# W's low pieces by VectorE, P7's bank in halves, another first load order, in a factorization kernel of seven products

## The chip, the cores and the metric

The kernel runs on one core of a Trainium2 chip. The metric is the device time of one execution in microseconds, the median of several. The core has TensorE for matrix products (PE in the profile, its weight loads PEld), VectorE (DVE), ScalarE (ACT), GpSimd (POOL) and SyncE (SP), each with an instruction stream of its own, and 16 DMA engines that they share. SBUF is the on-chip memory; PSUM is the small memory into which TensorE writes, in banks.

## The reference

A factorization machine: a linear layer and, for each of 512 outputs, the pairwise interaction of 64 embeddings. All of it is float32.

```python
# x 1024x512, weight 64x512x512, lin_w 512x512, lin_b 512
out_lin = x @ lin_w.T + lin_b
xv = jnp.einsum('bf,efm->bem', x, weight)
zp = jnp.einsum('bf,efm->bem', jnp.square(x), jnp.square(weight))
interaction = 0.5 * jnp.sum(jnp.square(xv) - zp, axis=1)
return out_lin + interaction
```

The second product needs no einsum of its own: summed over the embeddings it is x² times the column sums of W², one product of the size of the linear layer.

## The kernel before, in words

**Seven products.** Each large product is cut into 2 x 2 blocks and computed with seven products of blocks instead of eight. P1 to P7 are these products; X's operands are the blocks A11, A12, A22 and the sums R5, R6, R7, R3 (`OPERAND`), W's are the blocks w11, w21, w22, a sum w12 that takes w22 in, and T, which takes in one more block for each of P5, P6 and P4 (`RHS`, `load_more`, L596). There are 32 stages h, two for each of 16 groups of embeddings, and seven products in each. `ORDER = (1, 6, 2, 3, 7, 5, 4)` is their order within a stage, where 5 belongs to the next one.

**Three passes.** TensorE's full fp32 product is slow, its fp32r form is faster but cuts the operands. So `split` (L612) makes three pieces of a block of W: H, the block scaled and cut; L, what H leaves of it; K, a difference of the two. `x_pieces` (L471) does the same with X, once. A product is H by H and L by L, the "front" (8 matmuls of 128x512 for a half), then an operation on the bank that scales it and adds what another product left (`stt`, L349, or a scaling at L712), then the "back", K by K (4 matmuls), which TensorE's order puts `LAG = 4` slots later. In the first stage the products in `PLAIN` are done in fp32, without pieces. A product has two halves, each in a bank pair of its own out of four.

**Who makes a piece.** H is always a copy by ScalarE (`act`, L343), K a GpSimd operation (`pool`, L361). L is, by the table `SPLIT`, either a ScalarE copy and a GpSimd subtraction ("POOL"), or a ScalarE copy and an accumulating DMA that GpSimd issues ("DMA"), or one VectorE operation on two SBUF operands.

**The ends of a product.** P1 and P5: ScalarE copies the bank to p1 or p5. P6: VectorE makes w = bank + p5 (`dve`, L355). P2, P3, P4, P7: `finish` (L663): ScalarE squares the bank, VectorE reduces the squares over the embeddings of the stage into `acc` (L368). P7 also gives w = bank - p5, which P4 needs. The squares of W are ScalarE's `wsq` and a VectorE reduction `w_sum`. After every second stage the sums are transposed and stored.

**Head and tail.** The linear layer goes first, through the same seven products in fp32 (`one_level`, L485; P1 and P2 by `by_k`, L494, the rest L507), behind loads of x (`load_x`, SyncE's queue) and lin_w (`load_lw`, most on ScalarE's queue) and four matmuls of zeros. Then W's stages begin with P5 of stage 0. The tail is the product of x² with the sums of W², again by `one_level`, with VectorE adding the banks into the output tiles (`into`, L833).

**What sets the order.** The program is a list of operations with reads and writes. `Plan.forward` (L140) walks it with the cost of each operation (`plan.add`) and gives every engine a fixed order: TensorE by the keys (slots) of the products, the others by the latest time at which an operation may end, SyncE's loads no sooner than `AHEAD` before that. `Plan.order` (L117) repeats the walk `ROUNDS` times with changed deadlines and keeps the best. VectorE operations whose operands both lie in SBUF are marked `both`; the planner lets them and GpSimd's tensor operations take turns, and where it held one back the order between the two engines is made a dependency. DMAs of W's blocks are issued by SyncE (L375), accumulating ones by GpSimd (L380).

Of the kernel before, what the change touches and what calls it, by code (L numbers as in the profile page):

```python
# [33 lines left out]
PE, DVE, ACT, POOL, SP = "PE", "DVE", "ACT", "POOL", "SP"  # L34
# [3 lines left out]
class Plan:  # L38
    HOP = 0.3
    OWN = 0.05  # L40
    AHEAD = 50.0
    ROUNDS = 60
    SEED = 0
    DEPTH = 8
    YIELD = 0.0

# [27 lines left out]
    def deadlines(self, chain):  # L74
# [11 lines left out]
        while stack:  # L86
            o = stack.pop()
            latest = t if o.latest is None else o.latest
            cost = min(o.costs.values()) + o.move + o.land + self.HOP
# [50 lines left out]
    def forward(self, chain):  # L140
# [6 lines left out]
        done, late, nxt, wire, held = [], 0.0, 0, [9.0], None  # L147
# [5 lines left out]
        def ready(o, e=None):  # L153
            at = self.HOP
            for d in o.deps:
                own = ops[d].engine == e and not ops[d].move
                at = max(
                    at, ops[d].end + (self.OWN * (e != PE) if own else self.HOP * (e != NONE))
                )
            return at  # L160

        def ends(e, o, at):
            free[e], o.end, running[e] = at, at + o.land, o
# [3 lines left out]
            for t in (at, o.end, o.end + self.OWN, o.end + self.HOP):  # L167
                heapq.heappush(times, t)
# [6 lines left out]
        def pick(e, now):  # L175
# [23 lines left out]
        while len(done) < len(ops):  # L199
            now = heapq.heappop(times)  # L200
            moved = True
            while moved:
                moved = False
                for e in pending:
# [9 lines left out]
                    if e == PE:  # L214
                        nxt += 1
                        late = max(late, now - o.latest)
                    cost = o.costs[e]
                    o.start, o.engine = now, e
                    tensor = e == POOL and not o.move
                    if e == DVE and o.both and free[POOL] > now + 0.05 and not running[POOL].move:  # L220
                        held, free[e], o.end = o, float("inf"), float("inf")
                    elif tensor and held is not None and held.latest < o.latest + self.YIELD:
                        ends(DVE, held, now + held.costs[DVE])
                        o.after, held = held, None
                        ends(e, o, o.after.end + self.HOP + cost)
# [15 lines left out]
def kernel(  # L241
# [7 lines left out]
):  # L249

# [90 lines left out]
    def act(o, i, func, reads, writes, size=1024, scale=1.0, bias=0.0):  # L341
# [3 lines left out]
        plan.add({ACT: 0.14 + 0.92 * size / 1024}, emit, reads, writes)  # L345

    def stt(o, i, scalar, j, op, reads, writes, size=512, both=False, cost=None):
# [3 lines left out]
        plan.add({DVE: cost or 0.14 + 1.08 * size / 1024}, emit, reads, writes, both=both)  # L351

    def dve(o, a, b, sub, reads, writes, size=512, both=False):
# [3 lines left out]
        plan.add({DVE: 0.14 + 1.08 * size / 1024}, emit, reads, writes, both=both)  # L357

    def pool(o, a, b, sub, reads, writes, size=1024):
# [3 lines left out]
        plan.add({POOL: 0.15 + 2.35 * size / 1024}, emit, reads, writes)  # L363

    def reduce(o, i, reads, writes):
        plan.add(
            {DVE: 1.21},
# [6 lines left out]
    def dma(o, i, reads, writes, move=1.75, on=(SP,)):  # L374
        plan.add(dict.fromkeys(on, 0.45), lambda e: queues[e].dma_start(o, i), reads, writes,  # L375
                 land=2.0, move=move)

    def dma_add(o, i, reads, writes, move=2.75):
        plan.add(
            {POOL: 0.95}, lambda _: nc.gpsimd.dma_start(o, i, accum_op=ALU.add),  # L380
            tuple(reads) + tuple(writes), writes, land=2.5, move=move,
        )
# [20 lines left out]
    def load_x(n, k, lo, hi, at):  # L403
        r, q = quads[n]
        half = H // 2
        nc.sync.dma_start(
            buf[n][:, k, lo * half:hi * half],
            x_src[:, q * KH + k, r * H + lo * half:r * H + hi * half],
        )
        for u in range(lo, hi):  # L410
            landing((n, k, u), at)
# [9 lines left out]
    load_x("A11", 0, 0, 1, 3.5)  # L421
    load_lw(nc.scalar, [0], 0, 3.5)
    load_x("A11", 0, 1, 2, 3.9)
    load_lw(nc.scalar, [1], 0, 5.2)
    load_x("A11", 1, 0, 2, 5.0)
    load_lw(nc.scalar, [2, 3], 0, 7.2)
    load_x("A12", 0, 0, 2, 6.4)
    load_x("A12", 1, 0, 2, 7.4)
    load_lw(nc.sync, [0, 1], 1, 8.4)
    load_lw(nc.sync, [2, 3], 1, 9.2)  # L430
    for at, (n, k) in enumerate((("A22", 0), ("A22", 1), ("A21", 0), ("A21", 1))):
        load_x(n, k, 0, 2, 10.0 + 0.8 * at)
    nc.scalar.dma_start(bias[:], lin_b)
    landing("bias", 9.5)
    nc.scalar.preload_act_table(AF.Square)

    def a_parts(*names):
        return tuple((n, k, u) for n in names if n in quads for k in range(KH) for u in range(2)) + tuple(
# [46 lines left out]
    def one_level(p, rhs, left, bank, first, key, by_k=False):  # L485
# [3 lines left out]
        if by_k:  # L489
            for at, (u, k) in enumerate(steps):  # L490
                for half in range(2):
                    def emit(_, u=u, k=k, half=half):
                        cols = slice(half * H // 2, (half + 1) * H // 2)
                        nc.tensor.matmul(  # L494
                            buf[bank[u]][:, cols], b[:, k, ts(u, P)], a[:, k, cols],
                            start=first and k == 0 and half == 0, stop=k == KH - 1,
                            skip_group_check=True,
                        )

                    names = (a_names[2 * k + half],) + (b_names[k],)  # L500
                    plan.add({PE: WHOLE / 2}, emit, names + (bank[u],), (bank[u],),
                             key=key + 0.1 * at + 0.05 * half)
            return
        for u in range(2):
            def emit(_, u=u):
                for k in range(KH):
                    nc.tensor.matmul(  # L507
                        buf[bank[u]], b[:, k, ts(u, P)], a[:, k, :], start=first and k == 0,
                        stop=k == KH - 1, skip_group_check=True,
                    )  # L510

# [8 lines left out]
    f1, f4, f3, f2 = four()  # L520
# [32 lines left out]
    one_level(6, lin_rhs, lhs, f2, False, -960)  # L553
# [5 lines left out]
    lin_copy("L12", f2, 1, -1.0)  # L559
# [3 lines left out]
    one_level(7, lin_rhs, lhs, f2, False, -940)  # L563
    lin_add("L22", f2, True)
    lin_store("L22", 1, 1)
    lin_add("L21", f2, False)
# [29 lines left out]
    def load_more(h, n, q):  # L596

        o = now[h, n]
        if h:
# [28 lines left out]
    def prepare(h, p):  # L628
# [28 lines left out]
        return n if not h and p in PLAIN else split(n, SPLIT[p] if h else POOL)  # L657
# [5 lines left out]
    def finish(h, p, half, bank):  # L663
        row, col = {2: (0, 0), 3: (0, 1), 4: (1, 0), 7: (1, 1)}[p]
        sq, a = square(), acc_name[h // NCB]
        act(buf[sq], buf[bank], AF.Square, both_of(bank), (sq,))
        m, b = (2 * col + h % NCB) * MI, row * NJ + 2 * half
        reduce(buf[a][:, b:b + 2, m:m + MI], buf[sq], (sq,), ((a, b // 2, m),))

    def product(h, p):  # L670
        ops, plain = prepare(h, p), not h and p in PLAIN
        for half in range(2):
# [3 lines left out]
            def mm(x, w, j, first, bank=bank, half=half):  # L676
                for k in range(KH):
                    nc.tensor.matmul(buf[bank, j], buf[x][:, k, ts(2 * half + j, P)],  # L678
                                     buf[w][:, k, :], start=first and k == 0, stop=k == KH - 1,
                                     skip_group_check=True)  # L680

            addend = {6: "p1", 2: "p1", 3: "w", 7: "w", 4: "w"}.get(p)
# [236 lines left out]
```

## Time and profile before

| what | value |
|---|---|
| three runs | 1297.63, 1298.60, 1299.33 us (median 1298.6) |
| profiled execution | 1299.58 us, its span 1297.6 us |
| mean granted TensorE clock | 0.999 of full speed |
| matmuls (PE) | 1280.1 us busy, 99%, x5484 |
| VectorE (DVE) | 1086.7 us, 84%, x954 |
| ScalarE (ACT) | 1011.9 us, 78%, x1071 |
| GpSimd (POOL) | 1095.3 us, 84%, x590 |
| DMA | 200.25 MB; GpSimd's queue 101.72 MB |

The span runs from the first to the last instruction; the time of the execution has 2.0 us more. A row of a group has the line, engine, operation, tiles written and read, the number of instructions after x, and then busy time, mean duration in ns, and idle time before it with the releaser. A DMA row gives the queue, the number, KB of each and the median time from issue to landing. A record of TensorE is one pass over 512 columns; an fp32 matmul has two records. DVE durations run over the start of the next instruction by about 0.1 us, so the distance of two starts is what an operation costs on its engine.

### The profile page before, as it was taken

To read this page: it belongs to the slowest core of one execution; us is meant where nothing else is said; L and a number is where in the kernel's file an instruction comes from. 1 tells how busy PE (TensorE), PEld (TensorE's weight loads), DVE (VectorE), ACT (ScalarE), POOL (GpSimd) and SP (SyncE) were. 2 spreads that over 40 slices of the span, in tenths; PEclk is the share of its full clock that TensorE was granted. 3 is DMA by queue.
4 is the path that set the end of the run, shared out by engine and by line. 5 is a ranking of instruction groups with operands and counts; after the bars stand their busy time and mean duration, and the time that the engine had idled before them with its cause. 6 is when DMAs were issued, how large, how long until landed. Compare 5 with 4: busy or idle time off the path is not lost.

```text
span 1297.6 us, 15705 instructions
## 1 busy us (share of the span) xinstructions
PE 1280.1 (99%) x5484; PEld 1026.0 (79%) x5484; DVE 1086.7 (84%) x954; ACT 1011.9 (78%) x1071; POOL 1095.3 (84%) x590
## 2 busy tenths in 40 slices
PE   8999999999999999999999999999999999999997
PEld 4668888888888888888888888888888888888873
DVE  4699888888888888888888888888888889888884
ACT  5568788788777888877888887788888788888872
POOL 3659898898888899889889888888988888998891
PEclk9999999999999999999999999999999999999999
DMA  6366676757667666677766666767667676766866
GB/s 226 97 164 160 155 170 150 158 129 154 163 155 167 142 152 145 149 163 164 162 147 143 153 151 161 167 145 161 133 148 168 147 162 152 169 131 144 184 130 150
DMA packets 75998, 200.25 MB, mean 154 GB/s; under 512 B 23824, under 2 KB 25104, under 8 KB 75920
## 3 DMA queue, kind: packets, MB, share of 16 engines
q0 software_dynamic: 28512, 101.72, 44.0%
q1 hardware_dynamic: 45552, 94.91, 22.6%
q10 hardware_dynamic: 1856, 2.62, 0.6%
q8 instruction: 43, 0.70, 0.2%
q14 instruction: 35, 0.29, 0.1%
HBM read 158.34 MB, written 6.29 MB: 127 GB/s over the span
## 4 chain that ended last, share of the span: by engine, by line
PE 92%; DMA 3%; DVE 2%; ACT 1%; issue 1%; POOL 1%; SPq 0%; DVEq 0%; ACTq 0%; POOLq 0%
PE bank L678 89%; PE bank L507 3%; DMA T<-weight 1%; DMA w<-weight 1%; DMA w<-xT 0%; PE bank L494 0%; DVE w L355 0%; POOL pL L361 0%; ACT sq L343 0%; ACT wsq L343 0%; POOL pK L361 0%; ACT pL L343 0%; DVE bank L355 0%; ACT bank L343 0%; DVE bank L349 0%
## 5 line engine op out<-in xcount | busy, mean ns | idle before, releaser
L361 POOL TENSOR_TENSOR pK<-pH,pL 128x1024 fp32r<-128x1024 f32 x221 | 560.1, 2554 | 19.8 <-PE bank L678 10.8
L343 ACT ACTIVATE sq<-bank 128x1024 f32<-128x1024 f32 x256 | 261.5, 1022 | 112.8 <-DVE w L355 52.2
L368 DVE TENSOR_REDUCE acc<-sq 128x16 f32<-128x1024 f32 x256 | 306.9, 1211 | 10.7 <-ACT sq L343 10.7
L361 POOL TENSOR_TENSOR pL<-w,pL 128x1024 fp32r<-128x1024 f32 x95 | 240.3, 2530 | 13.8 <-ACT pL L343 11.8
L361 POOL TENSOR_TENSOR pL<-T,pL 128x1024 fp32r<-128x1024 f32 x64 | 155.0, 2422 | 97.2 <-ACT pL L343 95.7
L349 DVE SCALAR_TENSOR_TENSOR bank<-bank,w 128x1024 f32<-128x1024 f32 x190 | 233.0, 1226 | 3.4 <-PE bank L678 3.4
L355 DVE TENSOR_TENSOR w<-bank,p 128x1024 f32<-128x1024 f32 x128 | 156.7, 1224 | 54.6 <-PE bank L678 52.4
L349 DVE SCALAR_TENSOR_TENSOR bank<-bank,p 128x1024 f32<-128x1024 f32 x126 | 154.4, 1226 | 44.9 <-ACT p L343 35.9
L343 ACT ACTIVATE pL<-T 128x1024 fp32r<-128x1024 f32 x95 | 100.9, 1062 | 83.5 <-issue 44.2
L343 ACT ACTIVATE pL<-w 128x1024 fp32r<-128x1024 f32 x126 | 133.8, 1063 | 36.0 <-issue 29.6
L368 DVE TENSOR_REDUCE w_sum<-wsq 128x16 f32<-128x1024 f32 x128 | 155.2, 1213 | 7.9 <-ACT wsq L343 7.2
L343 ACT ACTIVATE wsq<-w 128x1024 f32<-128x1024 f32 x128 | 134.7, 1052 | 2.7 <-DVE w_sum L368 2.6
L343 ACT ACTIVATE p<-bank 128x1024 f32<-128x1024 f32 x128 | 130.1, 1018 | 8.4 <-PE bank L678 6.9
L343 ACT ACTIVATE pH<-w 128x1024 fp32r<-128x1024 f32 x126 | 133.0, 1055 | 0.0
L712 DVE TENSOR_SCALAR bank<-bank 128x1024 f32<-128x1024 f32 x62 | 76.4, 1232 | 54.8 <-PE bank L678 54.7
L343 ACT ACTIVATE pH<-T 128x1024 fp32r<-128x1024 f32 x95 | 100.0, 1052 | 0.0
L380 POOL DMA_DIRECT2D T<-weight x93 | 99.4, 1069 | 0.0
L678 PE MATMUL bank<-pH,X3H 128*128 128x512 f32 x256 | 78.9, 389 | 1.0 <-DVE w L355 1.0
L678 PE MATMUL bank<-pH,X7H 128*128 128x512 f32 x256 | 79.2, 390 | 0.4 <-ACT sq L343 0.3
L678 PE MATMUL bank<-pH,X5H 128*128 128x512 f32 x256 | 79.4, 391 | 0.0
L678 PE MATMUL bank<-pH,X2H 128*128 128x512 f32 x248 | 76.5, 389 | 2.7 <-ACT pH L343 2.7
L678 PE MATMUL bank<-pL,X7L 128*128 128x512 f32 x256 | 78.9, 389 | 0.0
(116 smaller groups left out, 2550.1 us busy)
## 6 DMA issues: line engine op xcount, KB each, us to landing
w<-weight SPq DMA_DIRECT2D x128, 512.0 KB, 5.6
T<-weight POOLq DMA_DIRECT2D x93, 512.0 KB, 7.4
T<-weight SPq DMA_DIRECT2D x32, 512.0 KB, 3.6
pL<-T POOLq DMA_DIRECT2D x31, 512.0 KB, 6.1
pL<-w POOLq DMA_DIRECT2D x31, 512.0 KB, 5.2
w<-weight POOLq DMA_DIRECT2D x31, 512.0 KB, 5.3
accd<-turned SPq DMA_DIRECT2D x64, 32.0 KB, 5.0
p<-lind SPq DMA_DIRECT2D x4, 512.0 KB, 4.7
```

The source lines that it names most:

```text
L343: nc.scalar.activation(o, i, func, bias=bias, scale=scale)
L349: return nc.vector.scalar_tensor_tensor(o, i, scalar, j, ALU.mult, op)
L355: return (nc.vector.tensor_sub if sub else nc.vector.tensor_add)(o, a, b)
L361: return (nc.gpsimd.tensor_sub if sub else nc.gpsimd.tensor_add)(o, a, b)
L368: lambda _: nc.vector.tensor_reduce(o, i.rearrange("p a (m e) -> p a m e", e=E), axis=AX.X, op=ALU.add),
L380: {POOL: 0.95}, lambda _: nc.gpsimd.dma_start(o, i, accum_op=ALU.add),
L507: nc.tensor.matmul(buf[bank[u]], b[:, k, ts(u, P)], a[:, k, :], start=first and k == 0, stop=k == KH - 1, skip_group_check=True,)
L678: nc.tensor.matmul(buf[bank, j], buf[x][:, k, ts(2 * half + j, P)], buf[w][:, k, :], start=first and k == 0, stop=k == KH - 1, skip_group_ ...
L712: plan.add({DVE: 1.2}, lambda _, o=o: nc.vector.tensor_scalar(o, o, 1 + U, None, ALU.mult), names, names)
```

## The change

- **W's pieces.** L of P5, P3 and P6 is made by VectorE. Before, P5 and P3 had it by accumulating DMA and P6 by GpSimd. No L of W is made by DMA. In stage 0 all go by GpSimd (`FIRST`).
- **The first stage.** P4 leaves `PLAIN` and goes in three passes. The sums of W's blocks in stage 0 are accumulating DMAs as in the other stages, not GpSimd additions (`MORE`).
- **X's pieces.** L and K of P1, P2 and P4 are ScalarE copies with accumulating DMAs; those of P5, P6, P3 and P7 stay on VectorE. X is no longer scaled up by S, so the squares and some sums take a scale instead.
- **P7's bank** ends in halves: ScalarE squares half 0 while VectorE makes w of half 1, then VectorE half 0, and ScalarE half 1.
- **The first loads** are whole 256 KB blocks of x on SyncE's queue and pairs of lin_w on ScalarE's; the bias is the last on SyncE's. lin_w's second half was on SyncE's queue, and the bias on ScalarE's.
- **Linear part.** P1 and P2 use whole 512-column matmuls and banks of their own; VectorE adds P2 to P1's copy. ScalarE's copy of P1's bank into P2's goes away. The tail does the same: P1 is added into the output tile, and P2 at the end from its own bank.
- **The planner** gets other costs for nearly all operations, a `TAIL` for each engine and a shorter `HOP`, a shorter lead for loads before 70 us (`EARLY`), no accumulating DMA more than 25 us ahead of its deadline (`SOON`), and ties some early transfers to a TensorE instruction (`mark`).

```diff
-PLAIN = (1, 2, 4)
+PLAIN = (1, 2)
-SPLIT = {**dict.fromkeys(range(1, 8), "POOL"), 5: "DMA", 3: "DMA"}
+SPLIT = {**dict.fromkeys(range(1, 8), POOL), 5: DVE, 3: DVE, 6: DVE}
+MORE = True
+X_SPLIT = {5: DVE, 6: DVE, 3: DVE, 7: DVE, 1: "DMA", 2: "DMA", 4: "DMA"}
+FIRST = dict.fromkeys(range(1, 8), POOL)
...
-    HOP = 0.3
-    OWN = 0.05
+    HOP = 0.06
+    TAIL = {"PE": 0.17, "DVE": 0.09, "ACT": 0.11, "POOL": 0.05, "SP": 0.0, "": 0.0}
     AHEAD = 50.0
+    EARLY = 70.0, 20.0
...
+    SOON = 25.0
...
-                if e == SP and o.latest - self.AHEAD > now + 1e-6:
-                    heapq.heappush(times, o.latest - self.AHEAD)
+                ahead = self.EARLY[1] if now < self.EARLY[0] else self.AHEAD
+                if e == SP and o.latest - ahead > now + 1e-6:
+                    heapq.heappush(times, o.latest - ahead)
                     return None
+                if e == POOL and o.move and o.latest - self.SOON > now + 1e-6:
+                    heapq.heappush(times, o.latest - self.SOON)
+                    continue
...
+                    if o.move and o.emit and mark and now < self.EARLY[0] and now > max(
+                        ready(o, e) + 0.3, free[e] + 0.1
+                    ):
+                        o.after = mark
...
-    load_x("A11", 0, 0, 1, 3.5)
-    load_lw(nc.scalar, [0], 0, 3.5)
-    load_x("A11", 0, 1, 2, 3.9)
-    load_lw(nc.scalar, [1], 0, 5.2)
-    load_x("A11", 1, 0, 2, 5.0)
-    load_lw(nc.scalar, [2, 3], 0, 7.2)
-    load_x("A12", 0, 0, 2, 6.4)
-    load_x("A12", 1, 0, 2, 7.4)
-    load_lw(nc.sync, [0, 1], 1, 8.4)
-    load_lw(nc.sync, [2, 3], 1, 9.2)
+    load_x("A11", 0, 3.9)
+    load_lw(nc.scalar, [0, 1], 0, 3.9)
+    load_x("A11", 1, 5.2)
+    load_lw(nc.scalar, [2, 3], 0, 5.6)
+    load_x("A12", 0, 7.4)
+    load_lw(nc.scalar, [0, 1], 1, 7.8)
+    load_x("A12", 1, 8.2)
+    load_lw(nc.scalar, [2, 3], 1, 8.8)
...
-    nc.scalar.dma_start(bias[:], lin_b)
-    landing("bias", 9.5)
+    nc.sync.dma_start(bias[:], lin_b)
+    landing("bias", 13.5)
...
-        act(buf[h], buf[n], AF.Copy, a_parts(n), (h,), scale=S * TRIM)
-        stt(buf[l], buf[n], S, f32(h), ALU.subtract, a_parts(n) + (h,), (l,), 1024, True)
-        stt(buf[k], f32(h), -U, f32(l), ALU.add, (h, l), (k,), 1024, True)
+        act(buf[h], buf[n], AF.Copy, parts, (h,), scale=TRIM)
+        if X_SPLIT[i] == "DMA":
+            act(buf[l], buf[n], AF.Copy, parts, (l,), scale=-TRIM)
+            dma_add(f32(l), buf[n], parts, (l,))
+            act(buf[k], buf[n], AF.Copy, parts, (k,), scale=-U * TRIM)
+            dma_add(f32(k), f32(l), (l,), (k,))
+        else:
+            dve(buf[l], buf[n], f32(h), True, parts + (h,), (l,), 1024, True)
+            stt(buf[k], f32(h), -U, f32(l), ALU.add, (h, l), (k,), 1024, True)
...
     one_level(1, lin_rhs, lhs, f1, True, -1000, True)
-    for u in range(2):
-        act(buf[f2[u]], buf[f1[u]], AF.Copy, (f1[u],), (f2[u],), 512)
-    one_level(2, lin_rhs, lhs, f1, False, -990, True)
     lin_copy("L11", f1, 0, 1.0)
+    one_level(2, lin_rhs, lhs, f2, True, -990, True)
+    lin_add("L11", f2, False)
     lin_store("L11", 0, 0)
...
-        if h:
+        if h or MORE:
             dma_add(buf[o], src(h, q), (), (o,))
...
-        return n if not h and p in PLAIN else split(n, SPLIT[p] if h else POOL)
+        return n if not h and p in PLAIN else split(n, SPLIT[p] if h else FIRST[p])
...
+        if p == 7:
+            n, p5 = value["w", h, half], value["p5", h, half]
...
+            def square_of(k):
+                act(buf[sq][:, k], buf[bank, k], AF.Square, ((bank, k),), ((sq, k), (bank, k)),
+                    512, scale=S)
+
+            def rest_of(k):
+                dve(buf[n, k], buf[bank, k], buf[p5, k], True, (p5, (bank, k)),
+                    ((n, k), (bank, k)))
+
+            square_of(0)
+            rest_of(1)
+            rest_of(0)
+            square_of(1)
+            used(sq, (sq, 0), (sq, 1))
+        else:
+            act(buf[sq], buf[bank], AF.Square, both_of(bank), (sq,), scale=S)
...
-            if p == 7:
-                n, p5 = value["w", h, half], value["p5", h, half]
-                dve(buf[n], o, buf[p5], True, (p5, *names), (n,), 1024)
...
     for u in range(2):
-        act(buf[f2[u]], buf[f1[u]], AF.Copy, (f1[u],), (f2[u],), 512, -1.0)
+        into(o_name[0, 0], f1, False, u)
...
-    one_level(2, right, left, f1, False, key + 20)
+    one_level(2, right, left, f2, True, key + 20)
     for u in range(2):
-        into(o_name[0, 0], f1, False, u)
+        into(o_name[0, 0], f2, False, u)
         store(0, 0, u)
```

More of the change, by code (lines that the diff above doesn't have):

```diff
@@ L224, in forward @@
                         o.after, held = held, None
-                        ends(e, o, o.after.end + self.HOP + cost)
+                        ends(e, o, free[DVE] + 0.15 + cost)
                     elif tensor and held is None and free[DVE] > now and running[DVE].both:
@@ L490, in one_level, with emit @@
             for at, (u, k) in enumerate(steps):
[L491 to L502, printed above, removed]
+                def emit(_, u=u, k=k):
+                    return nc.tensor.matmul(
+                        buf[bank[u]], b[:, k, ts(u, P)], a[:, k, :], start=first and k == 0,
+                        stop=k == KH - 1, skip_group_check=True,
+                    )
+                plan.add({PE: WHOLE}, emit, (a_names[k], b_names[k], bank[u]), (bank[u],),
+                         key=key + 0.1 * at)
             return
@@ L885 @@
                 ),
-                reason="the port that VectorE and GpSimd share",
+                reason="the order of transfers, or of two engines at the port that they share",
             )
```

116 lines of the change are left out of this document (59 added, 57 removed).

## The prediction

> **What bounds the kernel now.** I read the page's totals and its chain first, then the costliest groups, then the windows, and last the places where TensorE waits.
>
> ```profile
> span 1297.6 us, 15705 instructions
> PE 1280.1 (99%) x5484; PEld 1026.0 (79%) x5484; DVE 1086.7 (84%) x954; ACT 1011.9 (78%) x1071; POOL 1095.3 (84%) x590
> PE 92%; DMA 3%; DVE 2%; ACT 1%; issue 1%; POOL 1%; SPq 0%; DVEq 0%; ACTq 0%; POOLq 0%
> L361 POOL TENSOR_TENSOR pK<-pH,pL 128x1024 fp32r<-128x1024 f32 x221 | 560.1, 2554 | 19.8 <-PE bank L678 10.8
> L361 POOL TENSOR_TENSOR pL<-w,pL 128x1024 fp32r<-128x1024 f32 x95 | 240.3, 2530 | 13.8 <-ACT pL L343 11.8
> L343 ACT ACTIVATE pL<-T 128x1024 fp32r<-128x1024 f32 x95 | 100.9, 1062 | 83.5 <-issue 44.2
> L368 DVE TENSOR_REDUCE acc<-sq 128x16 f32<-128x1024 f32 x256 | 306.9, 1211 | 10.7 <-ACT sq L343 10.7
> ```
>
> TensorE is 92% of the chain that ended last. The other engines follow it; they cost time only where their product comes late. So the time falls by fewer TensorE passes or by removed waits, and taking work off GpSimd, ScalarE and the DMA queues is worth nothing by itself. By stage (span, busy time of PE, PEld, DVE, ACT, POOL; clock, DMA share, GB/s):
>
> ```profile
> 80.00:100.00 20.00, 17.28 (x72) 13.18 (x71) 19.84 (x18) 12.65 (x14) 11.28 (x8) 1.00 0.95 240
> 500.00:600.00 100.00, 100.00 (x443) 82.47 (x442) 84.92 (x75) 81.59 (x87) 90.28 (x49) 1.00 0.69 152
> ```
>
> In the steady part TensorE has no gap. VectorE has 15% left and GpSimd 10%. At 80 to 100 us VectorE and the DMA engines are full and TensorE is not.
>
> The waits of TensorE (start, duration, what ran, idle time before):
>
> ```profile
> 4.33 2.25 PE L494 MATMUL bank<-w,p 128*128 128x256 f32 x8
> 8.18 1.53 PE L494 MATMUL bank<-w,p 128*128 128x256 f32 x6 [1.60 <-DMA w<-xT]
> 10.38 0.70 PE L494 MATMUL bank<-w,p 128*128 128x256 f32 x2 [0.67 <-ACT bank L343]
> 11.75 0.48 PE L494 MATMUL bank<-w,p 128*128 128x256 f32 x1 [0.67 <-ACT bank L343]
> 15.82 0.70 PE L494 MATMUL bank<-w,p 128*128 128x256 f32 x2 [0.78 <-ACT wsq L343]
> 61.23 0.73 PE L678 MATMUL bank<-pH,X3H 128*128 128x512 f32 x2 [1.02 <-DVE w L355]
> 94.77 0.73 PE L678 MATMUL bank<-pH,X2H 128*128 128x512 f32 x2 [2.72 <-ACT pH L343]
> 520.51 0.62 PE L678 MATMUL bank<-pH,X3H 128*128 128x512 f32 x2
> ...
> 525.95 0.39 PE L678 MATMUL bank<-pH,X7H 128*128 128x512 f32 x1
> ```
>
> The first five waits are the linear part (3.72 us), the next two the first two stages. Between the last two rows lie one product's 24 matmuls in 5.44 us: 0.227 us each, so a stage of 168 takes 38.1 us. The chain gives the fp32 matmul, the load that TensorE waited for first, and the two pieces behind the stall at 94.77 (start, duration, engine):
>
> ```profile
> 1.21 0.43 SPq L406
> ...
> 1.69 6.35 DMA w<-xT
> ...
> 16.52 17.17 PE bank L507 x40
> ...
> 83.64 8.98 DMA w<-weight
> ...
> 93.68 1.05 ACT pH L343
> ```
>
> Forty records, two for each of 20 matmuls, take 17.17 us: 0.858 us each.
>
> **The linear part.** Its 28 matmuls are 24.03 us of work; counted from 4.33 they could end at 28.36, and end at 16.52 + 17.17 = 33.69. The excess is the 3.72 us of waits and about 1.6 us of halved matmuls and hand-overs. The change removes the two bank copies between P1 and P2 (2 x 0.67), the bank that P4 waited for (0.78) and the halves. What remains is the loads (KB, us from issue to landing):
>
> ```profile
> w<-xT SPq DMA_DIRECT2D x5, 256.0 KB, 6.4
> p<-lin_wT ACTq DMA_DIRECT2D x2, 128.0 KB, 3.1
> w<-xT SPq DMA_DIRECT2D x2, 128.0 KB, 3.2
> p<-lin_wT ACTq DMA_DIRECT2D x1, 256.0 KB, 7.1
> ```
>
> The block that TensorE waited for until 1.69 + 6.35 = 8.04 was the third issue of SyncE and becomes its second, 0.43 us earlier: 7.6 us. Behind it lie 26 matmuls, 22.3 us, so the end comes at 29.9 if the rest is there, and near 30.4 if it lands as late as before. I take -3.1 us. The bounds: if the first two blocks of each queue share the wires and both land at 8.0, everything lies behind that and the end is 8.0 + 24.0 = 32.0, -1.1 us after a hand-over of 0.6. If 256 KB land as the 128 KB did, 28.5 to 29: -4.6 us. The bias, last now, is read by ScalarE's copies of the banks; they come later than before, but TensorE does not wait for the first of them, since P1 and P2 have banks of their own.
>
> The Trainium skill (DMA: Bandwidth & Descriptors, section "Issuing engines are not separate DMA queues") says that queues of several engines end on the same 16 DMA engines. The rows agree: two 128 KB pieces that were alone took 3.1 to 3.2 us, 256 KB behind them 6.4 to 7.1. By it alone the upper bound, 32.0, would be the end.
>
> **P4 of the first stage in three passes.** Eight fp32 matmuls (6.86 us) become 24 (5.44): -1.42 us. It asks for H, L, K of a T, and for X4's pieces, by some 65 us; GpSimd is 78% or less busy there (15.58 of 20 in the row of 60 to 80 us, which a later fence shows), so they hide. If not, P4 waits for one GpSimd operation, 2.5 us.
>
> **The stalls at 61 and 94 us.** The first comes from VectorE, late by two operations that stood at the port that it shares with GpSimd (start, duration):
>
> ```profile
> 51.75 2.67 POOL L361 TENSOR_TENSOR pK<-pH,pL 128x1024 fp32r<-128x1024 f32 x1
> 52.07 3.44 DVE L349 SCALAR_TENSOR_TENSOR X3L<-w,X3H 128x1024 fp32r<-128x1024 f32 x1
> 34.92 1.22 DVE L349 SCALAR_TENSOR_TENSOR X6L<-sq,X6H 128x1024 fp32r<-128x1024 f32 x1
> 39.66 1.21 DVE L349 SCALAR_TENSOR_TENSOR X7L<-w,X7H 128x1024 fp32r<-128x1024 f32 x1
> 39.82 3.28 POOL L361 TENSOR_TENSOR pL<-w,pL 128x1024 fp32r<-128x1024 f32 x1 [1.16 <-DVE X6K L349]
> 60.00:80.00 20.00, 18.98 (x73) 13.57 (x73) 18.51 (x17) 13.25 (x14) 15.58 (x8) 1.00 0.22 54
> ```
>
> X3L needed 1.2 us and took 3.44: it waited for pK, begun 0.32 us before, to end at 54.42. X6L, with GpSimd idle, took 1.22. GpSimd in its turn took 3.28 instead of 2.5 beside X7L. The change takes six such VectorE operations (L and K of X1, X2, X4) away and gives them to ScalarE and accumulating DMAs: over 7 us of VectorE between 40 and 100 us, against a stall of 1.02. The second stall is a load of W issued at 83.64, behind a VectorE reduction that was late; with VectorE 7 us earlier it is issued earlier, and the 3.7 us of both go. Late next, by the order of the instructions, is P4 of the second stage, 0.25 us at most. Against it: ten accumulating DMAs of 512 KB more in this stretch, where the wires are 0.95 full at 80 to 100 us but 0.22 at 60 to 80. Bounds: -3.74 (both gone and nothing behind them) and +1 (neither gone, and a third one as long as the first). I take -3.7.
>
> **The steady part.** Per stage VectorE has 28 operations of 1.13 to 1.14 us from start to start; 84.92 of 100 is 32.3 of 38.1 us. It gets three Ls, and P7's two operations become four halves. Rows for these:
>
> ```profile
> 498.92 1.23 DVE L355 TENSOR_TENSOR w<-bank,p 128x1024 f32<-128x1024 f32 x1 [0.37 <-PE bank L678]
> 500.06 1.21 DVE L368 TENSOR_REDUCE acc<-sq 128x16 f32<-128x1024 f32 x1
> 500.24 1.03 ACT L343 ACTIVATE sq<-bank 128x1024 f32<-128x1024 f32 x1 [0.75 <-DVE w L355]
> 1291.55 1.88 DVE L355 TENSOR_TENSOR p<-p,bank 128x512 f32<-128x512 f32 x3 [1.54 <-PE bank L507]
> 1293.35 0.69 DVE L355 TENSOR_TENSOR p<-p,w 128x512 f32<-128x512 f32 x1
> ACT sq L343 <- DVE w L355: 52.2, 59, 1.2
> ```
>
> 500.06 - 498.92 = 1.14 for a whole operation; (1293.35 - 1291.55) / 3 = 0.60 for a half. So 32.3 + 3 x 1.14 + 4 x 0.60 - 2 x 1.14 = 35.8 of 38.1 us: 2.2 us are left for standing at the port. An L that meets a GpSimd operation at its start waits its whole length (X3L: 2.3 us), one that meets none waits nothing. In the order of instructions one L a stage meets a free port, one the middle of pK (about 1.05) and one its first half (about 1.4): 2.45 in all. But such a wait ends at a fixed time, the end of pK; if VectorE comes 0.3 us later it waits 0.3 us less. So 35.8 + 2.45 is not 0.2 us too much in each stage; what counts is the chain behind the fixed point: the back pass of P6, pK on GpSimd (2.55 by its row), L, ten VectorE operations, the w half and the ScalarE half, and then TensorE's P4 front in that bank. I make its slack 0.1 us in stages with the transposition of the sums and 0.5 in the others. P7's halves shorten its end: w (1.14) and the square (1.03) went one after the other, 59 waits of ScalarE in the last row, now they overlap by halves, two times 0.60 on either engine, about 1.2 instead of 2.2 us. I take +1.5 us for 31 stages (0.05 each); bounds 0 (the window of 500 to 600 has no gap to win back) and +6 (0.2 each).
>
> What goes: three ScalarE copies (3 x 1.06), one GpSimd subtraction of 2.5 us and 62 accumulating DMAs with their issue on GpSimd. All lie on engines with room and bring nothing by themselves, except that GpSimd leaves the port free more often, 84% busy instead of 90% (2.5 of 38.1 us), the issues not counted.
>
> **The tail.** After the last matmul VectorE has five operations instead of four, since P2 is no longer added to P1 in the bank: +0.6 us by the row at 1293.35. Bounds 0 and +1.2.
>
> **The sum.** -3.1 - 1.42 - 3.7 + 1.5 + 0.6 = -6.1 us. The profiled execution took 1299.58 us, 2.0 more than its span, and 1.0 more than the median, 1298.6. So 1293.5 in a profiled execution, and **1292.4** as a median; 1289.5 to 1296 for this case alone.
>
> **Rivals.** (1) VectorE becomes the bound, and the kernel slower. Place: the chain from pK to P4's front. If the slack that I read as 0.1 is -0.3 us, each of 31 stages is 0.3 longer, +9.3: with the gains of 8.2 and the tail's 0.6 the time is 1300.3, no change, and from there on it is slower. If each L waits half a GpSimd operation more than I think and nothing catches it, 0.75 us a stage, +23 us: 1314. For it: VectorE 94% busy before any wait, and three operations each stage of a kind that twice took 3.4 us. Against it: the fixed ends. Chance 0.15.
>
> The Trainium skill (Perfetto Trace Analysis, section "Optimizing Scalar/DVE Operations") says that moving work between GpSimd and VectorE might not help, as they share a port. Here X3L and X7L agree; by it alone this rival would be the forecast.
>
> (2) The sums of W come late. If VectorE's two-operand operations hold the port while GpSimd wants to issue accumulating DMAs, each sum lands up to 1.1 us later. The row below has ten places where ScalarE already waits for a T:
>
> ```profile
> ACT pL L343 <- DMA T<-weight: 17.6, 10, 2.7
> ```
>
> If all ten reach TensorE, +11 us: 1303. Chance 0.04. The Trainium skill (SBUF — State Buffer, box "The DVE blocks DMA trap (SWDGE)" in "SBUF: two separate sides") states the mechanism for VectorE's copies; no row here shows an issue held by VectorE.
>
> (3) The gain is smaller: the loads share the wires (2 us less) and one of the two early stalls stays or moves (1 to 3.7), or the chain costs 0.1 to 0.2 a stage: 1296 to 1301. Chance 0.13.
>
> (4) The gain is larger: loads as quick as the 128 KB pieces (1.5 us more), no loss in the steady part (1.5) and none in the tail (0.6): 1288.8 and a little to either side. Chance 0.08. That P7's halves do not overlap (ScalarE's order puts the second far behind) costs nothing: the serial form kept up.
>
> **The numbers.** The forecast has 0.60. The range, 1288 to 1301, holds it, case 3 and a little of case 4. A measurement can tell about 0.2%, 2.6 us: faster is below 1296.0 (0.60 + 0.08), the same up to 1301.2 (0.13), slower beyond (0.15 + 0.04).
>
> **What would show it.** The first stage's P5 near 30 us; no wait of 1 us or more on TensorE at 55 to 105 us; TensorE full from 200 to 1260 us with VectorE at 92 to 96% there, single Ls at 1.2 to 2.8 us; five VectorE operations behind the last matmul. Wrong: repeated waits of TensorE for ScalarE's square or VectorE's w in the steady part, waits for T, or a linear part that ends at 32.

## The result, and the profile after

The changed kernel takes 1331.93 us (median of five, 1329.82 to 1333.03) against 1299.33 us: a ratio of 1.0246, 95% interval 1.0229 to 1.0262. It is slower by 32.6 us; the forecast was 1292.4, faster by 6. The page of after, its totals and its chain:

```profile
span 1331.2 us, 15608 instructions
PE 1297.3 (97%) x5476; PEld 1024.0 (77%) x5476; DVE 1244.2 (93%) x1109; ACT 947.4 (71%) x1046; POOL 976.1 (73%) x505
DVE 66%; issue 14%; PE 13%; ACT 6%; POOL 1%; DMA 0%; DVEq 0%; ACTq 0%; POOLq 0%
```

The chain has turned over: TensorE was 92% of it and is 13%; VectorE is 66%. The window of 500 to 600 us, and the waits that are new:

```profile
500.00:600.00 100.00, 97.73 (x425) 79.03 (x424) 95.42 (x87) 74.55 (x83) 76.52 (x39) 1.00 0.55 127
...
ACT sq L358 <- DVE w L370: 41.3, 63, 2.5
DVE w L370 <- ACT sq L358: 39.3, 60, 1.4
PE bank L711 <- ACT sq L358: 21.6, 56, 0.8
```

TensorE ran 443 passes in this window before and now 425. Before, ScalarE's square waited for VectorE's w 59 times; now VectorE's w also waits for ScalarE's square, 60 times, and TensorE for the square 56 times. All 56 are P4, going into the bank that P7 leaves; such repeated waits are the prediction's own sign of being wrong. One such end of P7 in the timelines of VectorE, ScalarE and TensorE:

```profile
620.60 0.68 DVE L370 TENSOR_TENSOR w<-bank,p 128x512 f32<-128x512 f32 x1
621.37 0.60 ACT L358 ACTIVATE sq<-bank 128x512 f32<-128x512 f32 x1 [0.62 <-DVE w L370]
622.01 0.69 DVE L370 TENSOR_TENSOR w<-bank,p 128x512 f32<-128x512 f32 x1 [0.73 <-ACT sq L358]
622.82 0.59 ACT L358 ACTIVATE sq<-bank 128x512 f32<-128x512 f32 x1
...
622.10 1.07 PE L711 MATMUL bank<-pK,X7K 128*128 128x512 f32 x4
623.46 0.73 PE L711 MATMUL bank<-pH,X4H 128*128 128x512 f32 x2 [0.29 <-ACT sq L358]
```

The four half operations run one after the other: 620.60, 621.37, 622.01, 622.82, end at 623.41. That is 2.81 us; in the kernel before, the whole bank took from 498.92 to 501.27, 2.35 us. VectorE stands idle 0.73 us between its halves, since its order has nothing between them. P4 should have started at 622.10 + 4 x 0.227 = 623.01 and starts at 623.46.

Where the time went, by three places of TensorE's timeline: P5 of the third stage, P4 of the last, and the end. Rows of after (before: 33.12, 111.22 and 1256.48 for the first stage's P5, the third's and the last P4):

```profile
31.40 0.80 PE L711 MATMUL bank<-pH,X5H 128*128 128x512 f32 x1
...
106.09 0.39 PE L711 MATMUL bank<-pH,X5H 128*128 128x512 f32 x1
...
1288.78 0.39 PE L711 MATMUL bank<-pH,X4H 128*128 128x512 f32 x1
```

The head is 5.1 us faster, the steady part 37.4 slower (1182.7 for 1145.3 us; the usual stage takes 39.43 us for 38.11), the tail 1.3 slower (42.4 for 41.1): together +33.6, the difference of the spans.

### The profile page after: what moved, and what is told of

Same layout as the page of the kernel before. It is cut to its first block, busy times and chain, and to the rows that moved or that the text cites. A ratio compares the mean times of both kernels' runs of the same rounds, so it can differ in the third digit from the quotient of the medians.

```text
span 1331.2 us, 15608 instructions
## 1 busy us (share of the span) xinstructions
PE 1297.3 (97%) x5476; PEld 1024.0 (77%) x5476; DVE 1244.2 (93%) x1109; ACT 947.4 (71%) x1046; POOL 976.1 (73%) x505
## 4 chain that ended last, share of the span: by engine, by line
DVE 66%; issue 14%; PE 13%; ACT 6%; POOL 1%; DMA 0%; DVEq 0%; ACTq 0%; POOLq 0%
DVE bank L364 18%; DVE acc L383 16%; DVE pL L364 12%; PE bank L711 9%; DVE w L370 8%; DVE w_sum L383 7%; DVE bank L749 5%; ACT sq L358 3%; PE bank L519 3%; ACT wsq L358 2%; PE bank L508 1%; POOL pK L376 0%; ACT pH L358 0%; DMA p<-lin_wT 0%; ACT bank L358 0%
## 5 line engine op out<-in xcount | busy, mean ns | idle before, releaser
L358 ACT ACTIVATE sq<-bank 128x1024 f32<-128x1024 f32 (+1 forms) x320 | 271.6, 849 | 176.6 <-PE bank L711 130.3
L370 DVE TENSOR_TENSOR w<-bank,p 128x512 f32<-128x512 f32 (+1 forms) x192 | 164.6, 861 | 39.8 <-ACT sq L358 39.3
L395 POOL DMA_DIRECT2D T<-weight x96 | 93.7, 976 | 127.5 <-DVE pL L364 110.9
L358 ACT ACTIVATE p<-bank 128x1024 f32<-128x1024 f32 x128 | 130.3, 1020 | 30.9 <-PE bank L711 30.8
L358 ACT ACTIVATE pL<-w 128x1024 fp32r<-128x1024 f32 x95 | 101.0, 1063 | 61.8 <-PE bank L711 46.6
L711 PE MATMUL bank<-pH,X4H 128*128 128x512 f32 x256 | 86.2, 418 | 21.9 <-ACT sq L358 21.6
L364 DVE SCALAR_TENSOR_TENSOR pL<-pH,T 128x1024 fp32r<-128x1024 f32 x62 | 98.1, 1582 | 0.3 <-ACT pH L358 0.3
L376 POOL TENSOR_TENSOR pL<-T,pL 128x1024 fp32r<-128x1024 f32 x34 | 82.6, 2428 | 17.7 <-ACT pL L358 17.7
L711 PEld LDWEIGHTS bank<-pH,X4H 128*128 128x128 f32 x256 | 43.3, 188 | 53.6 <-ACT sq L358 47.2
L364 DVE SCALAR_TENSOR_TENSOR pL<-pH,w 128x1024 fp32r<-128x1024 f32 x31 | 82.5, 2662 | 0.0
L711 PE MATMUL bank<-pL,X4L 128*128 128x512 f32 x256 | 79.8, 393 | 0.0
```

The lines of the kernel that those rows point to most:

```text
L358: nc.scalar.activation(o, i, func, bias=bias, scale=scale)
L364: return nc.vector.scalar_tensor_tensor(o, i, scalar, j, ALU.mult, op)
L370: return (nc.vector.tensor_sub if sub else nc.vector.tensor_add)(o, a, b)
L376: return (nc.gpsimd.tensor_sub if sub else nc.gpsimd.tensor_add)(o, a, b)
L395: {POOL: 0.62}, lambda _: nc.gpsimd.dma_start(o, i, accum_op=ALU.add),
L711: made = nc.tensor.matmul(buf[bank, j], buf[x][:, k, ts(2 * half + j, P)], buf[w][:, k, :], start=first and k == 0, stop=k == KH - 1, skip ...
```

## The experiments

**First set: take parts back.** Theory A: P7's halves in series and three Ls together overfill VectorE. *whole* ends P7's bank in one piece; *old_split* restores the table; *whole_old_split* both; *told* leaves the halves but puts each down as holding the whole bank, so that the planner knows the series, and lists VectorE's w of half 1 before the square of half 0, the order in which the timeline of after already has the two engines.

```diff
# whole: finish() as before, and behind it
+            if p == 7: dve(buf[n], o, buf[p5], True, (p5, *names), both_of(n), 1024)
# old_split
+SPLIT = {**dict.fromkeys(range(1, 8), POOL), 5: "DMA", 3: "DMA"}
# told: writes of square_of and rest_of
-((sq, k), (bank, k))            ((n, k), (bank, k))
+((sq, k), *both_of(bank))       ((n, k), *both_of(bank))
```

> The changed kernel with P7's bank ended whole again (one square of 128x1024 by ScalarE, one w by VectorE), the rest of the change kept. Theory A: in the changed kernel the halves run one after the other and VectorE stands idle between its two (0.73 us twice a stage); with about 35.8 us of operations and 2.4 us at the shared port this makes 39.4 us a stage. Without halves VectorE needs 38.1 to 38.2 us, so the stage falls to 38.1-38.4 and the time to 1293-1303 us. Theory B: the three Ls at the port are enough to bind; then the stage stays at 38.8 or more and the time at 1316 us or more.

1324.01 us, 1.0178 (1.0163 to 1.0193). A's 1293-1303 is missed; the time and the stages, most of 38.9 to 39.6 us, lie where theory B put them. Only 8 us came back. TensorE now waits for VectorE's w instead, 18 of these 20 times with P4:

```profile
PE bank L692 <- DVE w L370: 17.0, 20, 1.1
```

So the whole bank is late as well, where the planner is not told that its two readers go one after the other.

> The changed kernel with the old table SPLIT (L of P5 and P3 by accumulating DMA, of P6 by GpSimd), P7's halves kept. Theory A (the sum on VectorE decides): VectorE needs 32.4 + 1.5 of idle in the halves = 34 of 38.1 us, TensorE binds again, 1294-1302 us. Theory C: the four steps of P7's halves, 2.86 us instead of 2.54 for the whole bank, hold up P4 whatever VectorE has to do; then a stage keeps 0.3 to 1.3 us over 38.1 and the time is 1306-1332 us.

1355.42 us, 1.0428 (1.0404 to 1.0452): 23 us slower yet, which no theory had. The first stage takes 42.5 us for 34.7 in after, with one wait of TensorE of 6.5 us for ScalarE's p.

> The changed kernel with both taken back: P7's bank whole and the old table SPLIT; what stays is the head, the tail, the first stage and the planner's costs. Every theory that puts the loss into the steady part expects the gain of the head alone (5.1 us at the third stage in the two traces) and the tail's 1.3 us: 1293-1297 us. If the planner's new costs cost something themselves, 1300 or more.

1353.25 us, 1.0406 (1.039 to 1.0422). So something in what stays loses with the old table (the first stage, 42.8 us, has the same wait of 6.5); the planner's constants were the suspect.

> The changed kernel, but the planner is told that P7's four half operations follow one another (each is put down as writing the whole bank), so that it can put other operations between VectorE's two. Theory A in its idle part: the 2 x 0.73 us that VectorE stands idle are filled, the stage falls from 39.4 to 38.3-38.8 us, 1299-1316 us. If the idle time between the halves is only where lateness from the port shows, nothing is won: 1328-1334 us.

1315.82 us, 1.0123 (1.0103 to 1.0142): half of the loss goes without a single operation changed, only by the order. The upper end of A's range for it, 1316, just holds it. The window, and the one stall that each stage keeps:

```profile
500.00:600.00 100.00, 99.17 (x436) 81.17 (x435) 97.82 (x86) 73.71 (x81) 75.79 (x38) 1.00 0.55 123
...
614.33 0.74 PE L711 MATMUL bank<-pH,X4H 128*128 128x512 f32 x2 [0.42 <-ACT sq L358]
```

VectorE now fills its gaps with a reduction. A stage takes 38.86 us, 0.75 over 38.11, with a recorded wait of 0.42. So the four steps still do not fit into the 2.72 us (12 passes) from P7's last back matmul to P4's front in the same bank. Once the first half of P4 is late, the second has its time.

**Second set: one part alone, and the whole bank told.** Theory D: the end of P7 decides.

```diff
# whole_told: order and both holders of the bank put down
+        if p == 7:
+            dve(buf[n], buf[bank], buf[p5], True, (p5, *both_of(bank)),
+                (*both_of(n), *both_of(bank)), 1024)
+        act(buf[sq], buf[bank], AF.Square, both_of(bank), (sq, *both_of(bank)), scale=S)
# b_halves, b_split, b_newplan: the kernel before with P7's halves alone, the new SPLIT alone,
# the planner's new constants and costs alone (without the early ties)
```

> The changed kernel with P7's bank whole, VectorE's w first, and the planner told that ScalarE's square of any bank comes after it and that both hold the bank. Theory D (the two engines read a PSUM bank one after the other, and the time from P7's last back matmul to P4's front in the same bank is 2.72 us): w and square need 0.2 + 1.14 + 0.1 + 1.03 = about 2.5 us if VectorE stands ready, four halves about 2.95; so the stall of 0.75 us a stage that is left when the halves are told to the planner goes, the stage falls to 38.1-38.3 us and the time to 1290-1300 us. Theory A (VectorE's sum with the three Ls binds): with 38.0 of 38.86 us busy there is no room to stand ready, the stage stays at 38.8 or more: 1314 us or more.

1307.19 us, 1.0069 (1.0052 to 1.0085): between D's range and A's. The stages from the thirteenth on mostly take 38.2 us, as D says; nine of the ten before take 38.9 to 40.5.

> The kernel before with only P7's bank in halves, as the changed kernel writes them. Theory D: four steps of some 0.7 us do not fit into 2.72 us, whatever VectorE has besides: at least one stall of 0.75 us a stage, 31 x 0.75 = 23 us, 1318-1332 us. Theory A: VectorE has room here (32.4 + 1.5 us), no loss: 1297-1303 us.

1331.48 us, 1.0252 (1.0237 to 1.0268). The halves alone, in a kernel whose VectorE is 82% busy, cost as much as the whole change, at the upper end of D's 1318-1332. A falls: no overfull VectorE is needed. The window, and the waits of VectorE and of TensorE (31 of the 32 with P4) for the square:

```profile
500.00:600.00 100.00, 97.94 (x427) 79.25 (x426) 84.17 (x80) 82.57 (x93) 88.20 (x47) 1.00 0.64 144
DVE w L355 <- ACT sq L343: 55.6, 53, 2.2
PE bank L700 <- ACT sq L343: 18.0, 32, 0.7
```

> The kernel before with only L of P5, P3 and P6 by VectorE. VectorE then has 35.7 us of operations a stage and 2 to 3 us at the port. Theory A: it binds or nearly so, a stage takes 38.4-39.5 us, 1307-1345 us. Theory D: it matters only where it keeps VectorE from standing ready at P7's end; with the old planner's margins 0 to 0.5 us a stage, 1297-1313 us.

1312.43 us, 1.0108 (1.0092 to 1.0124): the three Ls alone cost 14 us, within both ranges.

> The kernel before with only the planner's new constants and costs (HOP 0.06, TAIL, the costs of all helpers, SOON; without the early ties). Theory E: the new constants leave no margin between operations (0.06 us from one engine to the next where the traces show 0.2 from TensorE to VectorE and 0.1 elsewhere) and are a cause of their own; with old SPLIT and whole banks the changed kernel took 1353 us. Then 1320 us or more. Without theory E: 1295-1303 us.

1336.09 us, 1.0291 (1.0274 to 1.0308): theory E's 1320 or more. The new constants alone cost 38 us here.

In whole_told the late stages and the early ones differ most plainly in the L of w22 beside pK (DVE and POOL; a late stage, then an early one):

```profile
670.42 1.21 DVE L364 SCALAR_TENSOR_TENSOR pL<-pH,w 128x1024 fp32r<-128x1024 f32 x1
670.45 3.45 POOL L376 TENSOR_TENSOR pK<-pH,pL 128x1024 fp32r<-128x1024 f32 x1
...
278.61 0.86 POOL L395 DMA_DIRECT2D w<-weight  x1
279.03 3.97 DVE L364 SCALAR_TENSOR_TENSOR pL<-pH,w 128x1024 fp32r<-128x1024 f32 x1
279.22 2.69 POOL L376 TENSOR_TENSOR pK<-pH,pL 128x1024 fp32r<-128x1024 f32 x1
```

Where L comes first, pK takes 3.45 us (2.40 in the next one of that stage) and L 1.21; where GpSimd stands before it with a DMA issue and goes on to pK, L takes 3.97. In seven of the first eleven stages L takes 3.5 us or more, and each of these takes 39.5 to 40.5 us. The Trainium skill (SBUF — State Buffer, section "SBUF: two separate sides") calls the pair of ports an exclusive lock for the whole instruction; the two cases agree with it: GpSimd as the loser waits about 1.05 us, most of L's 1.21, and VectorE about 2.76 us, all of pK's 2.69. Whether the DMA issue held the port at 279.03 the trace does not say.

**Third set: two Ls, and the old constants.**

```diff
# two_ls: whole_told with
+SPLIT = {**dict.fromkeys(range(1, 8), POOL), 5: DVE, 6: DVE}
# old_plan, whole_told_old_plan: the changed kernel, or whole_told, with class Plan and the costs of
# the kernel before; head_alone: the same with the whole bank as in whole, and the old SPLIT
```

> The changed kernel with the planner's old constants and costs (HOP 0.3, the old cost of each helper, no SOON, no early ties), halves and the new SPLIT kept. If the new constants cost something of their own here too (theory E, +38 us when put alone into the kernel before), the time falls to 1305-1325 us. If the halves decide (33 us alone), it stays at 1325-1340 us.

1376.75 us, 1.0599 (1.0584 to 1.0613): beyond both ranges. The first stage takes 50.0 us, and nearly every later one 40.3, with two waits of 0.69 us of P4 for the square.

> The changed kernel with three parts taken back: P7's bank whole, the old SPLIT, the planner's old constants. What stays is the new loads, the linear part, the first stage in three passes with its pieces of X, and the tail. By the traces, the head of the changed kernel gains 5.1 us by its third stage and its tail loses 1.3: 1293-1297 us. If the accumulating DMAs of the first stage or the smaller scale cost later stages something, 1299 us or more.

1325.7 us, 1.021 (1.0196 to 1.0224). The old constants do not fit the new head: its first stage takes 50.4 us (35.5 in the kernel before), with waits of TensorE of 5.07 us for GpSimd's pL and 4.86 for ScalarE's pH. By the third stage's P5 that is 10 us of the loss; another 13 lie in the steady part (1158.5 for 1145.3 us), and what causes them was not followed up.

> The whole bank told to the planner, all three Ls by VectorE, the planner's old constants. If the new constants cost something even where the bank is told: 1293-1302 us (from 1307). If the old ones, with longer costs, see VectorE as too full (1.22 instead of 1.14 us for each operation), 1307-1325 us.

1337.97 us, 1.03 (1.0286 to 1.0314), beyond both ranges; the first stage takes 48.6 us here.

> The kernel with the whole bank told to the planner, and L of P3 back on GpSimd, so that VectorE makes two Ls a stage. In the run with three, ten early stages took 40.2 us, in each of which the L of w22 stood 2.7 us at the port, and later ones 38.2 us with none. Theory F (VectorE with three Ls has no room to come out of such a bad state quickly): with one L less all stages take 38.1-38.3 us, 1290-1296 us, faster than the kernel before. If the early loss has another cause, 1302 us or more.

1292.43 us, 0.9954 (0.9942 to 0.9967): faster than the kernel before by half a percent. Theory F is right: from the fourth stage on all take 38.2 us. The totals, the chain, the window and the three places:

```profile
PE 1278.2 (99%) x5476; PEld 1023.9 (79%) x5476; DVE 1152.3 (89%) x1014; ACT 966.5 (75%) x1013; POOL 1046.7 (81%) x536
PE 96%; DMA 1%; DVE 1%; ACT 0%; issue 0%; DVEq 0%; ACTq 0%
...
500.00:600.00 100.00, 100.00 (x442) 82.38 (x441) 91.79 (x80) 75.78 (x81) 84.06 (x43) 1.00 0.49 114
...
28.87 0.79 PE L696 MATMUL bank<-pH,X5H 128*128 128x512 f32 x1
...
101.80 0.39 PE L696 MATMUL bank<-pH,X5H 128*128 128x512 f32 x1
...
1248.70 0.39 PE L696 MATMUL bank<-pH,X4H 128*128 128x512 f32 x1
```

By the same places its head is 9.4 us faster than before, its steady part 1.6 slower and its tail 0.7 slower.

**Fourth set: is it the draw of the planner?** Nearly every part, taken alone, had lost. That could also mean that any new order loses against a lucky old one.

```diff
# before_seed, after_seed
-    SEED = 0
+    SEED = 1
# halves_two: the changed kernel, halves and all, with SPLIT of two_ls
# l53: whole_told with
+SPLIT = {**dict.fromkeys(range(1, 8), POOL), 5: DVE, 3: DVE}
```

> The kernel before, only the seed of the planner's draws changed from 0 to 1, so that every engine gets another order of the same operations. Theory G (the order of the kernel before is a lucky draw, and whatever is planned anew loses 14 to 40 us): 1312-1340 us. If the draw matters little and the parts have costs of their own: 1296-1304 us.

1302.74 us, 1.0023 (1.0014 to 1.0033).

> The changed kernel, only the planner's seed changed to 1. If its loss lies in the operations (P7's halves one after the other, three Ls at the port): 1325-1340 us, 39.2-39.6 us a stage. If it is the draw: anything from 1292 to 1345, and more than 10 us from 1332.

1329.66 us, 1.0235 (1.0218 to 1.0252), 39.42 us a stage. With one other draw for each kernel the difference is 2 to 3 us, not 30: theory G falls.

> The changed kernel with L of P3 back on GpSimd, everything else kept, the halves too. If the halves carry a loss of their own (four steps after one another at P7's end, not told to the planner): at least 0.75 us a stage over 38.1, 1314-1325 us. If the third L was the whole cause (VectorE too full): 38.1-38.4 us a stage, 1291-1300 us.

1330.92 us, 1.0243 (1.0228 to 1.0258), above both ranges and on the side of the halves. With the halves there is no gain from the third L's going: a stage takes 39.47 us, and in its second half of P4 TensorE waits for the square:

```profile
627.41 0.73 PE L711 MATMUL bank<-pH,X4H 128*128 128x512 f32 x2 [0.81 <-ACT sq L358]
```

So the halves are enough for the whole loss, with three Ls, with two, and with none (b_halves). But the parts do not add up: without the halves the changed kernel still takes 1324 us (whole), and 1307 with the order told.

> The whole bank told to the planner, L of P5 and P3 by VectorE and of P6 by GpSimd: two Ls a stage again, but w22's among them. If it is the number of Ls that counts: 1290-1296 us as with P5 and P6. If w22's L, which stood 2.7 us at the port behind a DMA issue and pK, is bad wherever VectorE makes it: 1298-1310 us.

1298.36 us, 0.9987 (0.9977 to 0.9996). That is on the border, 0.4 us inside the second range (w22's L bad wherever it is made), so the time does not settle it. The steady stages speak for the number of Ls: most take 38.1 to 38.4 us although w22's L takes 2.5 to 3.8 us nearly every time. l53 is slower than two_ls by its linear part (31.10 against 28.87), its third stage (41.3 against 39.6) and some 2 us elsewhere; the difference in the linear part comes and goes between runs with the same loads.

**Last: the constants, and the tail.** *b_newplan_told* adds the told bank to b_newplan; *two_ls_tail* puts the old tail into two_ls.

> The kernel before with the planner's new constants (+38 us alone) and with the order at the bank told (VectorE's w first, each of the two put down as holding the bank). If the new constants lose only because the planner takes two reads of one bank for simultaneous: 1296-1305 us, no stall of P4 in most stages. If the short HOP costs by itself at other places: 1315 us or more.

1347.55 us, 1.0377 (1.0356 to 1.0398): telling does not help here. P4 waits for the square 8 times instead of 30 in b_newplan, but 18.4 us in all instead of 14.4. The waits of this run show another place too:

```profile
POOL pK L371 <- DMA pL<-w: 50.5, 21, 5.6
...
ACT pL L353 <- DMA T<-weight: 45.3, 28, 3.5
```

Before, GpSimd waited for no DMA of pL<-w and ScalarE 17.6 us for T. The new constants issue an accumulating DMA no more than 25 us ahead of its deadline and put its issue at 0.62 us instead of 0.95 (its transfer at 3.1 instead of 2.75). Where L itself comes by such a DMA, as in the kernel before and in the two runs with the old table, what stands behind it may be late for that reason. This is argued from the waits, not shown; which of the constants it is was not tried.

> The fastest version (whole bank told, two Ls by VectorE) with the tail of the kernel before: P2 added to P1 in the bank again, four VectorE operations behind the last matmul instead of five. From X4 of the last stage to the end the kernel before needs 41.1 us, this version's parent 41.8: 0.6 us less, about 1291.8 us, if the prediction's term for the tail is right; the same or more if the earlier copy of the bank costs TensorE as much.

1292.8 us, 0.9947 (0.9935 to 0.996): no different from two_ls. The old tail, planned anew, also has five VectorE operations behind the last matmul.

## Why the prediction was wrong, by its own steps

**The step that failed** is in the steady part: P7's halves "now they overlap by halves", 1.2 instead of 2.2 us, and, under the rivals, that if they did not it "costs nothing: the serial form kept up". They follow one another, each waiting for the one before, and take 2.81 us instead of 2.35. The slack was 0.1 to 0.5 us by my own reading of the chain. The row with 59 waits of ScalarE for VectorE's w, which I quoted, showed that two reads of one bank stand in series, and I took it for an order that the halves would dissolve. In after the series has four steps, 63 waits of the square for w and 60 of w for the square; what in the program makes them wait was not looked into. Price: 33 us alone (b_halves), and 38 from two_ls to halves_two, which differ in the halves and in what the planner is told.

The Trainium skill (PSUM — Partial Sum Buffer, section "PSUM bank collisions raise a hardware error") says that two engines may not use one bank at once, reads against reads included, a bank being 2 KiB. By it the square of half 0 and w of half 1 could have run together, since each half is a bank. In this program they do not; with separate tiles for the halves it was not tried.

**Rival 1** named the right place, "the chain from pK to P4's front", and too small a size, at most 0.75 us a stage and 1314 us where it is 1.3 and 1332, with a chance of 0.15; its cause, Ls at the port, was the smaller part. The Ls cost 14 us alone and 15 over two of them (whole_told against two_ls). "2.45 in all" at the port was close for after: 62 Ls of T at 1.58 us and 31 of w22 at 2.66, less 1.22 each (an L that meets nothing), are 2.2 us a stage. w22's L waited longest. "Such a wait ends at a fixed time" did not keep seven early stages of whole_told, in which w22's L took 3.5 us or more, from taking 39.5 to 40.5 us.

**The linear part**, -3.1 (-1.1 to -4.6): -1.7 in after, -4.25 in two_ls (28.87 for 33.12), the loads the same. Of eleven traced runs with these loads and the new constants, five end at 28.8 to 29.0 and six at 30.9 to 31.4; both lie within the bounds. The landing of the loads is not what differs: in all eleven TensorE's first weight load waits 2.1 to 2.3 us for lin_w, until 5.1 to 5.2. The pace behind it is (the same stretch, 4 to 12 us, of after, then of two_ls):

```profile
5.08 7.14 PE L508 MATMUL bank<-w,p 128*128 128x512 f32 x10 [0.55 <-DMA p<-lin_wT]
5.14 7.13 PE L508 MATMUL bank<-w,p 128*128 128x512 f32 x16 [0.61 <-DMA p<-lin_wT]
```

In the slower six the first four to six passes start 0.83 us or more apart and those that follow soon 0.43; in the other five 0.43 holds from the second pass on. The profile's granted clock reads 1.00 there in both, and what sets the pace stays open. The prediction, which took 0.858 us for every matmul of two passes, had no term for it, and which pace an execution gets is luck. That the runs of one kernel fall into two groups some 2.3 us apart (two_ls: 1292.2 to 1292.4 and 1294.5 to 1294.7) fits this; it is not shown, as one execution of each is traced.

**P4 in three passes and the stalls at 61 and 94**, -1.42 and -3.7: right. In two_ls the first two stages take 34.76 and 38.17 for 35.50 and 42.60, -5.2 for -5.1. In after the first halved P7 takes a part back, a wait of P4 of 0.83 us at 75.55 us.

**The tail**, +0.6 (0 to 1.2): +0.7 in two_ls, +1.3 in after. **The steady part**, +1.5 (0 to 6), is the term that failed, and twice. Besides the halves, three Ls cost more than it allowed: whole_told, whose bank is whole and told, has +16.6 there (1161.9 for 1145.3 us). The +1.6 of two_ls belongs to a kernel with one L less, and that its 1292.4 is the number of the forecast is luck.

**Not weighed at all** was the planner. Its new constants cost 38 us in the kernel before, and the old ones at least 13 us of first stage in the changed one; I priced the operations and took the order as given. two_ls, which has the new constants, shows no such loss.

## What to carry to other kernels

Before halving an operation so that two engines share it, look whether the two already wait for one another in the trace: a wait of one reader for another can be an order that the halves keep, and here they only doubled its steps. Compare the length of the new chain with the time that the next user of the buffer leaves, here 2.72 us, not with the engines' load. And a planner that is not told of such an order puts other work into the gap that it believes to be there: 16 of the 32 us came back by telling it.

## What was not expected of the hardware

A wait of TensorE costs more than the row says. In told one recorded wait of 0.42 us a stage lengthens the stage by 0.75. At 614.33 two starts of matmuls lie 0.81 us apart instead of 0.227: the row counts its wait only from the end of the record before, and that record, 0.39 us long, runs over the next start. The start after it comes 0.34 us later, 0.11 too late. Both make 0.69 of the 0.75 us. In halves_two the recorded 0.81 costs 1.08 us in the same way, and the other half of P4 loses 0.24 more without a recorded wait, of 1.36 us in all.
